# A graph layer with 12522 gathers of 128 rows: six stretches of them are cut to 112, 96, 64, 105, 98 and 80 rows

## The chip, the core and the metric

The kernel runs on one core of one Trainium2 chip. The time is the device time of that core in microseconds; the kernel before takes 17915.2 us (median of 2 runs, 17912.69 and 17917.71). Its profiled execution took 18022.0 us.

The engines are named as the profile names them: PE is TensorE (its weight loads are PEld), DVE is VectorE, ACT is ScalarE, POOL is GpSimd, and SP is SyncE, which here only issues transfers. A `q` behind a name is the queue in which an engine issues transfers.

## The reference

A graph of 50000 nodes has 1650000 edges, sorted by their destination; one edge of each node is a loop to itself. A node carries 160 numbers (64 scalars and 32 vectors of 3), an edge carries 4 (`sh`). For each edge the row of its source node is combined with the edge's four numbers and five small weight matrices, the results are summed over the edges of each destination, and the sum goes through two more matrices, a ReLU, a residual and a layer norm:

```python
ss, vv = (s[src], v[src])
e0 = sh[:, 0:1]
e1 = sh[:, 1:4]
dot = jnp.einsum('eui,ei->eu', vv, e1)
out0 = C0 * (ss * e0 @ W1 + dot * INV3 @ W2)
p3 = (ss @ W3)[:, :, None] * e1[:, None, :] * INV3
p4 = jnp.einsum('eui,uw->ewi', vv * e0[:, :, None], W4) * INV3
p5 = jnp.einsum('eui,uw->ewi', jnp.cross(vv, e1[:, None, :]), W5) * INV6
out1 = C1 * (p3 + p4 + p5)
m = jnp.concatenate([out0, out1.reshape(-1, 3 * MUL1)], axis=1)
m_agg = jax.ops.segment_sum(m, dst, num_segments=n)
...
return x + jax.nn.relu(h)          # h: m_agg through Ws and Wv
...
x = _layernorm(x + _L0_gnn_ref(...), axis=-1)
```

## The kernel before

Everything up to the ReLU is linear in the gathered rows, so the kernel first sums, for each node and each of the edge's four numbers, the number times the source's row (4 x 160 sums a node), and multiplies with one combined matrix `BWk` afterwards.

**Units, groups, pairs, chunks.** 128 edges are a unit. For each unit, POOL gathers the 128 source rows of 640 bytes from HBM into one slice of the tile `xg` (line 398), one index in each partition. Six units (`G`) are a group; the destinations of a group lie within 32 consecutive nodes (`W`), since the edges are sorted. Two groups are a pair: 12 gathers, one `xg` tile, one `ps` tile. There are four `xg` tiles (pool `rows`), so the first gather of a pair waits until PE has read the pair four before. Twenty groups (`SG`) are a chunk, 120 gathers: for a chunk the sources, destinations and numbers of its edges are loaded (`load`), transposed so that the edges of a unit lie across the partitions (`place`), and the destinations are taken relative to the first node of their group (`rel`). `place` also keeps the least and the largest `rel` of each chunk in `extremes`, for a check at the end that all lay within the 32 nodes.

**A pair.** VectorE compares `rel` with 0 to 31 (`hot`, line 419) and multiplies with the edge's four numbers (`ha`, line 422): a matrix of 128 edges by 4 x 32. PE multiplies it with the gathered rows (line 447) and adds up six units in `ps`; the trace counts two matmul passes for each unit. VectorE turns `ps` in blocks of 32 (line 462) and adds it to the sums of the current segment of nodes, `ring`, at a column that depends on the data (line 471). When the last group that can touch a block of 128 nodes is done, five matmuls with `BWk` (line 776) and the norm finish it.

**Loops.** From the 101st group on (`NH` = 100) the edges are not read from the inputs but from a table `edges` that the kernel writes ahead of use, without the loops: `pack` takes rows of 1185 edges, 128 rows at a time (11 packs), moves the loops out with predicated copies on VectorE, and stores what is left. The loops' share is added node by node (`ask_own`, `set_own`). `reach` says how far in the table a chunk reads.

**What sets the order.** The engines' programs are written out in order (`manual_schedule`): the loop over the pairs issues the 12 gathers of a pair, then its matmuls, and between these, after each, a share of the other work (blocks, the next chunk, packs). A chunk's loads are issued three pairs ahead of the chunk that stands before it (`LEAD`). `near` estimates the destination of a group's first edge from its place in the list; from it follow the segments, the windows and the pairs after which each block can be finished.

Before, a group's first edge is simply `g * G * P`, 768 edges a group. The lines of the loads in the six stretches, of the gathers and of the matmuls are these:

Of the kernel before, what the change touches and what calls it, by code (L numbers as in the profile page):

```python
# [44 lines left out]
ALU = mybir.AluOpType  # L45
AX = mybir.AxisListType
# [4 lines left out]
P = 128  # L51
MUL0, MUL1 = 64, 32
D = MUL0 + 3 * MUL1
NK = 4
# [9 lines left out]
W = 32  # L64
# [4 lines left out]
SG = 20  # L69
# [10 lines left out]
ASK, OWN, QS, RUN = 8, 16, 8, 2  # L80
LEAD = 3

def plan(n_nodes, n_edges):

    nblk = 125
    assert n_nodes % nblk == 0
    assert W == FB
    nb = n_nodes // nblk
    again = 9

    per_unit = P * n_nodes / n_edges
# [10 lines left out]
    assert eh + (rows - 1) * row - n_nodes + eh * n_nodes / n_edges - far >= ngroups * group * P  # L102
    units = P * math.ceil(max(math.ceil(n_edges / P) + again - 1, math.ceil((eh + rows * row + 1) / P)) / P)
    return nblk, nb, again, group, units, ngroups, row, head, rows, far


@with_exitstack
def tile_gnn_resnorm(ctx: ExitStack, tc: tile.TileContext, x, src, dst, attr, W1, W2, W3, W4, W5, Ws, Wv, out, n_edges):
    nc = tc.nc
    N = x.shape[0]  # L110
    NBLK, NB, GA, G, NU, NG, L, NH, NR, FAR = plan(N, n_edges)
    EH = NH * G * P
    degree = n_edges / N

# [98 lines left out]
    cuts = sorted({0, NH, NG} | {round(i * NG / 10 / SG) * SG for i in range(10)})  # L213
# [5 lines left out]
    NSC = math.ceil(NG / SG)  # L219
    part_of = [next(i for i, (g0, g1) in enumerate(parts) if g0 <= s * SG < g1) for s in range(NSC)]  # L220
    off_of = [offs[i] for i in part_of]
    low = [max(math.floor(near(g)) - off_of[g // SG] - 1, 0) for g in range(NG)]
# [9 lines left out]
    with tc.tile_pool(name="once", bufs=1) as once, tc.tile_pool(name="raw", bufs=2) as rawp, \  # L232
# [20 lines left out]
        dq = nc.sync  # L253
# [3 lines left out]
        def load(s):  # L257

            g0 = s * SG
            ng = min(NG, g0 + SG) - g0  # L260
            u0, f0 = (g0 * G, g0) if s + 1 < NSC else ((g0 + ng) * G - P, g0 + ng - W)
            at = (g0 * G - u0, g0 - f0, ng)

            def fetch(to, what, c):

                rows = what.rearrange("(u i q) -> i u q", u=P // RUN, i=NK)
                dq.dma_start(to.rearrange("p (b r) q -> p b (r q)", r=RUN), rows)

            def fetch_first(to, what, c):

                firsts = what.rearrange("(g q) -> g q", g=W)[:, 0:1]
                with nc.allow_non_contiguous_dma(reason="one number of each group"):
                    dq.dma_start(to, firsts.unsqueeze(0).to_broadcast([NK, W, 1]))

            if g0 >= NH:
                C = 2 + NK
                if s * SG > NH:
                    f0 = g0 + ng - W
                    at = (at[0], g0 - f0, ng)
                p0, q0 = u0 * P - EH, f0 * G * P - EH  # L280
                r6 = rawp.tile([P, NK * W * C], F32, name="r6").rearrange("p (b e c) -> p b e c", b=NK, c=C)
                fd = rawp.tile([P, 1], F32, name="fd")
                fetch_first(fd, edges[0, q0 * C + 1:(q0 + W * G * P) * C + 1], C)
                fetch(r6.rearrange("p b e c -> p b (e c)"), edges[0, p0 * C:(p0 + P * P) * C], C)
# [61 lines left out]
        def place(cast_):  # L346
# [28 lines left out]
            if s:  # L375
# [15 lines left out]
        def gather(s, placed, u, n):  # L391
# [4 lines left out]
            begun_tiles[0] += 1  # L396
            for j in range(n):
                part = nc.gpsimd.indirect_dma_start(  # L398
                    out=xg[:, j, :], out_offset=None, in_=x,
                    in_offset=bass.IndirectOffsetOnAxis(ap=placed[0][:, u + j:u + j + 1], axis=0))  # L400
# [5 lines left out]
                rows.append((xg[:, j, :], filled[t][j], 16 * gathers[t][j], key))  # L406
            return rows

        idle, sent = [], []
# [32 lines left out]
        def group_sums(p, rows, ha):  # L442
# [1 line left out]
            ps = psA.tile([P, PG, D], F32, name="ps")  # L444
            fresh("ps")
            for j, (xr, sem, count, key) in enumerate(rows):
                mm = nc.tensor.matmul(ps[:, j // G, :], ha[:, j].rearrange("p k w -> p (k w)"), xr,  # L447
                                      start=j % G == 0, stop=j % G == G - 1)
                mm.wait_op(sem, count, "sem-ge")
                tc.declare_no_dep(mm.ins, group=key, reason="its own semaphore is waited for")  # L450
# [23 lines left out]
        C = 2 + NK  # L474
# [442 lines left out]

        def reach(s):

            end = min(NG, (s + 1) * SG) * G * P  # L920
            if s * SG < NH:
                return 0
            if s + 1 < NSC:
                end = max(end, (s * SG * G + P) * P)
            if s * SG == NH:
                end = max(end, (s * SG + W) * G * P)
            return end - EH

        packs, due = [], []
# [235 lines left out]
```

## Time and profile before

| | |
|---|---|
| time | 17915.2 us (median of 2 runs) |
| profiled execution | 18022.0 us, span 18020.3 us |
| POOL busy | 11866.1 us, 66% of the span |
| VectorE busy | 7478.3 us, 41% |
| PE busy, weight loads busy | 6860.2 us (38%), 6095.4 us (34%) |
| mean granted TensorE clock | 0.627 |
| gathers | 12522, mean 947 ns |
| transfer engines, the gathers' queue | 1026.60 MB, 23.5% of 16 engines' span |
| groups, pairs, chunks | 2087, 1044, 105 |

A group's row in the profile gives line, engine, operation and tiles (written <- read), the count, then busy time, the mean of one in ns, and the idle time of the engine just before these instructions with what ended most of it. "issue" means that the engine waited for nothing that the profile shows; "remote" that it was released by something that the profile does not show. A row of waits gives the total in us, how often, and the longest. A row of a timeline gives start and duration in us, and in square brackets the idle time before.

### The profile page before, as it was taken

The page shows a single profiled execution, that of the slowest core. Times are in us where ns is not written, and L with a number is a line of the kernel's source. Part 1 is how long each engine was busy: PE and PEld are TensorE (multiplying, and loading weights), DVE is VectorE, ACT ScalarE, POOL GpSimd, SP SyncE. Part 2 cuts the span into 40 slices and gives each one's busy share as a digit, 9 for nine tenths or more (in the row PEclk, how much of TensorE's full clock was granted, in tenths as well). Part 3 has the DMA queues.
Part 4 walks back from the last instruction along what each step waited for, and adds up shares of the span by engine and source line. Part 5 has one row for each costly group of instructions (what it writes and reads, how often), then busy time and mean ns, then how long its engine had stood idle before and what let it go on. Part 6 is the DMA issues. An engine that isn't in the chain of part 4 may idle for free. (4 is left out here: it accounts for less than half of the span.)

```text
span 18020.3 us, 93561 instructions
## 1 busy us (share of the span) xinstructions
PE 6860.2 (38%) x28971; PEld 6095.4 (34%) x28972; DVE 7478.3 (41%) x12038; ACT 171.6 (1%) x273; POOL 11866.1 (66%) x12535
## 2 busy tenths in 40 slices
PE   3333334333333333333333333333333333333433
PEld 2233333333333333333333333333333333333333
DVE  7344245334524442453344345434433452444232
ACT  0000000000000000000000000000000000000000
POOL 6566666666666666666666666666666666666666
PEclk6666666666666666666666666666666666666666
DMA  2222322322332233223223322332232233222222
GB/s 72 79 71 78 79 68 73 83 76 70 77 81 70 71 80 77 70 73 85 73 70 78 80 70 72 82 77 69 72 85 74 69 76 78 72 70 71 75 72 61
DMA packets 740962, 1341.57 MB, mean 74 GB/s; under 512 B 243310, under 2 KB 522674, under 8 KB 725894
## 3 DMA queue, kind: packets, MB, share of 16 engines
q0 software_dynamic: 601056, 1026.60, 23.5%
q1 hardware_dynamic: 138138, 308.06, 5.6%
q8 instruction: 231, 3.78, 0.1%
q14 instruction: 273, 2.24, 0.0%
q10 hardware_dynamic: 1264, 0.88, 0.0%
HBM read 1263.28 MB, written 71.42 MB: 74 GB/s over the span
## 5 line engine op out<-in xcount | busy, mean ns | idle before, releaser
L398 POOL DMA_INDIRECT xg<-in_x,si x12522 | 11862.6, 947 | 6108.8 <-issue 3663.5
L447 PE MATMUL ps<-xg,ha 128*128 128x160 f32 x25044 | 6282.8, 397 | 9643.7 <-issue 5600.4
L447 PEld LDWEIGHTS ps<-xg,ha 128*128 128x128 f32 x25044 | 5409.4, 267 | 10356.9 <-issue 10352.3
L462 DVE STREAM_TRANSPOSE sums<-ps 128x320 f32<-128x320 f32 x1044 | 527.0, 505 | 6249.8 <-remote 4712.4
L422 DVE TENSOR_TENSOR ha<-hot,pk 128x1536 f32<-128x1536 f32 x1044 | 1830.4, 1753 | 52.1 <-remote 11.0
L776 PE MATMUL phb<-BWk,ring 128*128 128x160 f32 (+1 forms) x3910 | 1176.4, 381 | 1441.0 <-issue 858.6
L184 DVE SCALAR_TENSOR_TENSOR y<-phb,xt 128x320 f32<-128x320 f32 x196 | 95.9, 489 | 3623.2 <-PE ps L447 2504.7
L776 PEld LDWEIGHTS phb<-BWk,ring 128*128 128x128 f32 (+1 forms) x3910 | 894.1, 258 | 1489.1 <-issue 886.9
L471 DVE TENSOR_TENSOR ring<-ring,sums 128x160 f32 x2087 | 684.5, 328 | 253.1 <-issue 158.6
L419 DVE TENSOR_TENSOR hot<-bank,rel 128x384 f32<-128x384 f32 x1044 | 570.6, 547 | 67.4 <-DMA xt<-in_x 67.3
L632 DVE COPY_PREDICATED prow<-marks,prow 128x2370 f32<-128x2370 int32 (+5 forms) x198 | 550.3, 2780 | 1.1
L766 DVE STREAM_TRANSPOSE ring<-xr 128x1280 f32<-128x1280 f32 x188 | 437.2, 2326 | 0.1
L632 DVE COPY_PREDICATED pra<-marks,pra 128x1580 f32<-128x1580 int32 (+5 forms) x198 | 378.8, 1913 | 0.0
L763 DVE TENSOR_TENSOR xr<-xr,bank 128x1280 f32<-128x1280 f32 x188 | 276.5, 1471 | 4.6 <-DVE bank L756 1.4
L194 ACT ACTIVATE rstd<-mv,eps_t 128x2 f32<-128x2 f32 x196 | 58.0, 296 | 16997.5 <-DVE mv L189 12612.7
L468 DVE TENSOR_TENSOR ring<-ring 128x196 f32<-128x196 f32 (+20 forms) x485 | 149.4, 374 | 1.8
L200 DVE TENSOR_SCALAR o<-y,mv,rstd 128x160 f32<-128x160 f32 x391 | 130.2, 374 | 10.9 <-remote 1.6
L629 DVE COPY_PREDICATED_SCALAR hit<-marks,none 128x395 int32 (+5 forms) x198 | 130.1, 657 | 10.9 <-DVE pri L627 3.2
L716 DVE MEMSET ring<- 128x1280 f32 (+1 forms) x98 | 119.3, 1218 | 23.1 <-issue 21.0
L188 DVE BATCH_NORM_STATS2 st<-y 128x6 f32<-128x160 f32 x391 | 121.7, 311 | 6.7
L630 DVE COPY_PREDICATED hit<-marks,pri 128x395 int32<-128x395 int32 (+5 forms) x198 | 118.5, 598 | 10.4 <-issue 2.2
L627 DVE TENSOR_TENSOR pri<-hit,marks 128x395 int32<-128x395 int32 (+11 forms) x198 | 113.5, 573 | 14.8 <-issue 3.2
(346 smaller groups left out, 1752.7 us busy)
## 6 DMA issues: line engine op xcount, KB each, us to landing
xg<-in_x,si POOLq DMA_INDIRECT x12522
xr<-in_x SPq DMA_DIRECT2D x93, 1280.0 KB
r<-edges SPq DMA_DIRECT2D x100, 384.0 KB
edges<-prow SPq DMA_DIRECT2D x1330, 27.8 KB
xt<-in_x SPq DMA_DIRECT2D x195, 160.0 KB
out<-o SPq DMA_DIRECT2D x195, 160.0 KB
pra<-in_attr SPq DMA_DIRECT2D x10, 2370.0 KB
selves<-mine SPq DMA_DIRECT2D x1328, 0.8 KB
```

The source lines that it names most:

```text
L200: nc.vector.tensor_scalar(o[:n, i], y[:n, i], mv[:n, i, 0:1], rstd[:n, i:i + 1], op0=ALU.subtract, op1=ALU.mult)
L398: part = nc.gpsimd.indirect_dma_start(out=xg[:, j, :], out_offset=None, in_=x, in_offset=bass.IndirectOffsetOnAxis(ap=placed[0][:, u + j:u ...
L419: idle[:] = [nc.vector.tensor_tensor(hot[:, :n], slotsP[:, 0:W].unsqueeze(1).to_broadcast([P, n, W]), rel[:, u:u + n].unsqueeze(2).to_broa ...
L422: nc.vector.tensor_tensor(ha[:, :n], hot[:, :n].unsqueeze(2).to_broadcast([P, n, NK, W]), pk[:, :, u:u + n].rearrange("p k u -> p u k").un ...
L447: mm = nc.tensor.matmul(ps[:, j // G, :], ha[:, j].rearrange("p k w -> p (k w)"), xr, start=j % G == 0, stop=j % G == G - 1)
L462: nc.vector.transpose(at[:, :ng], ps[:, :ng].rearrange("p g (b f) -> p g b f", f=FB))
L468: nc.vector.tensor_tensor(ring[k][:, b, :past], ring[k][:, b, :past], ring[k - 1][:, b, S:S + past], op=ALU.add)
L471: nc.vector.tensor_tensor(here, here, at[:, i], op=ALU.add)
L632: nc.vector.copy_predicated(what[:n, a:e], mi[:, r].unsqueeze(2).to_broadcast([n, e - a, what.shape[2]]), what[:n, a + d:e + d])
L763: nc.vector.tensor_tensor(xr[:, r], xr[:, r], sumP[:, r].unsqueeze(2).to_broadcast([P, r.stop - q, D]), op=ALU.mult)
L766: nc.vector.transpose(here[:, r], xr[:, r].rearrange("p q (b f) -> p q b f", f=FB))
L776: wrote("misc", nc.tensor.matmul(ph[:nb], ring[k][:, i, cols], BWk[:, i, :], start=i == 0, stop=i == ND - 1))
```

## The change

Of the chunks 8 to 14, 18 to 24, 28 to 34, 38 to 44, 48 to 54 and 58 to 64, a gather takes 112, 96, 64, 105, 98 and 80 edges in place of 128, on the first so many partitions; all other chunks keep 128. A group there has six times so many edges. The edges that these groups no longer take go to later groups: there are now 2320 groups, 1160 pairs, 116 chunks and 13920 gathers. `starts` holds each group's first edge. A short chunk's edges are loaded in two transfers: one for the full blocks of 32 edges in a unit, one for the rest (with edges behind the unit's end, which no one reads). The matmuls take the same first partitions; the one-hots and their products are still made for all 128.

```diff
+SIZES = (112, 96, 64, 105, 98, 80)
+
+
+def size_of(s):
+    i, j = divmod(s - 8, 10)
+    return SIZES[i] if 0 <= i < len(SIZES) and j < 7 else P
...
-    ngroups = math.ceil((n_edges - n_nodes + eh * n_nodes / n_edges + far) / (group * P))
...
+    starts = [0]
+    while starts[-1] < n_edges - n_nodes + eh * n_nodes / n_edges + far:
+        g = len(starts) - 1
+        starts.append(starts[-1] + group * (P if g < head else size_of(g // SG)))
...
     def near(g):
-        p = g * G * P
+        p = starts[g]
...
+        nc.vector.memset(extremes, 0.0)
...
             def fetch(to, what, c):
 
+                if size[s] < P:
+                    m = size[s] // W
+                    for i, what_ in ((slice(0, m), what[0:P * size[s] * c]), (slice(m, NK), what[m * W * c:])):
+                        by_unit = what_.rearrange("(u q) -> u q", u=P)[:, 0:(i.stop - i.start) * W * c]
+                        dq.dma_start(to[i.start * W:i.stop * W], by_unit.rearrange("u (i q) -> i u q", q=W * c))
+                    return
...
-            nc.vector.tensor_reduce(extremes[:, 0, s:s + 1], rel[:, :n], axis=AX.X, op=ALU.min)
-            begun.append(nc.vector.tensor_reduce(extremes[:, 1, s:s + 1], rel[:, :n], axis=AX.X, op=ALU.max))
+            nc.vector.tensor_reduce(extremes[:size[s], 0, s:s + 1], rel[:size[s], :n], axis=AX.X, op=ALU.min)
+            begun.append(nc.vector.tensor_reduce(extremes[:size[s], 1, s:s + 1], rel[:size[s], :n], axis=AX.X, op=ALU.max))
...
                 part = nc.gpsimd.indirect_dma_start(
-                    out=xg[:, j, :], out_offset=None, in_=x,
-                    in_offset=bass.IndirectOffsetOnAxis(ap=placed[0][:, u + j:u + j + 1], axis=0))
+                    out=xg[:size[s], j, :], out_offset=None, in_=x,
+                    in_offset=bass.IndirectOffsetOnAxis(ap=placed[0][:size[s], u + j:u + j + 1], axis=0))
...
-                mm = nc.tensor.matmul(ps[:, j // G, :], ha[:, j].rearrange("p k w -> p (k w)"), xr,
+                mm = nc.tensor.matmul(ps[:, j // G, :], ha[:xr.shape[0], j].rearrange("p k w -> p (k w)"), xr,
```

What this does to the order shows on POOL first. Before, its program is these rows from the end of the start-up on, nearly all in one run of gathers (`128x160` is partitions by numbers, `x` how many stand in a row):

```order
L803 IOTA quarter 128x4
L999 IOTA place 128x1185
L398 DMA xg<-in_x,si 128x160 x49
L505 IOTA at 1x1408
L398 DMA xg<-in_x,si 128x160 x12473
```

Now, from the same place up to the end of the third short stretch (line 398 has become 420):

```order
L825 IOTA quarter 128x4
L1021 IOTA place 128x1185
L420 DMA xg<-in_x,si 128x160 x49
L527 IOTA at 1x1408
L420 DMA xg<-in_x,si 128x160 x911
L420 DMA xg<-in_x,si 112x160 x840
L420 DMA xg<-in_x,si 128x160 x360
L420 DMA xg<-in_x,si 96x160 x840
L420 DMA xg<-in_x,si 128x160 x360
L420 DMA xg<-in_x,si 64x160 x840
```

Each short stretch is 840 gathers, with 360 full ones up to the next; the other three follow in the same way, and 6120 full ones stand at the end.

SP is the other engine whose program changes its form. At the load of chunk 8, the first short one, it had before (`fd` holds the destinations of the groups' first edges, `r` the chunk's edges, `xt` the node rows of two blocks, `sa` and `xr` what the loops need):

```order
L875 DMA out<-o 128x320
L273 DMA fd<-edges 128x1x1
L267 DMA r_4696<-edges 128x2x384
L709 DMA xt<-in_x 128x320
L746 DMA sa<-selves 128x1x64
L746 DMA xr<-in_x 128x1x2560
```

and now:

```order
L897 DMA out<-o 128x320
L295 DMA fd<-edges 128x1x1
L286 DMA r_4683<-edges 96x4x192
L286 DMA r_4683<-edges 32x4x192
L731 DMA xt<-in_x 128x320
L768 DMA sa<-selves 128x1x64
L768 DMA xr<-in_x 128x1x2560
```

The one transfer of the edges has become two, in runs of 192 numbers in place of 384, and what follows it stands one transfer later.

More of the change, by code (lines that the diff above doesn't have):

```diff
@@ L100, in plan @@
     rows = math.ceil((n_edges - eh) / row) + 2
-    ngroups = math.ceil((n_edges - n_nodes + eh * n_nodes / n_edges + far) / (group * P))
-    assert eh + (rows - 1) * row - n_nodes + eh * n_nodes / n_edges - far >= ngroups * group * P
+    starts = [0]
+    while starts[-1] < n_edges - n_nodes + eh * n_nodes / n_edges + far:
+        g = len(starts) - 1
+        starts.append(starts[-1] + group * (P if g < head else size_of(g // SG)))
+    assert size_of((len(starts) - 2) // SG) == P and len(starts) - 1 > head + SG
+    assert eh + (rows - 1) * row - n_nodes + eh * n_nodes / n_edges - far >= starts[-1]
     units = P * math.ceil(max(math.ceil(n_edges / P) + again - 1, math.ceil((eh + rows * row + 1) / P)) / P)
-    return nblk, nb, again, group, units, ngroups, row, head, rows, far
+    return nblk, nb, again, group, units, starts, row, head, rows, far
 @with_exitstack
@@ L110, in tile_gnn_resnorm @@
     N = x.shape[0]
-    NBLK, NB, GA, G, NU, NG, L, NH, NR, FAR = plan(N, n_edges)
+    NBLK, NB, GA, G, NU, starts, L, NH, NR, FAR = plan(N, n_edges)
+    NG = len(starts) - 1
     EH = NH * G * P
@@ L212, in tile_gnn_resnorm @@
     S = SB * P
-    cuts = sorted({0, NH, NG} | {round(i * NG / 10 / SG) * SG for i in range(10)})
+    cuts = sorted({0, NH, NG} | {round(i * NG / 10 / SG) * SG for i in range(10)}
+                  | {g for g in range(NH, NG, SG) if size_of(g // SG) != size_of(g // SG - 1)})
     parts = list(zip(cuts, cuts[1:]))
@@ L219, in tile_gnn_resnorm @@
     NSC = math.ceil(NG / SG)
+    size = [P if s * SG < NH else size_of(s) for s in range(NSC)]
     part_of = [next(i for i, (g0, g1) in enumerate(parts) if g0 <= s * SG < g1) for s in range(NSC)]
@@ L279, in load @@
                     at = (at[0], g0 - f0, ng)
-                p0, q0 = u0 * P - EH, f0 * G * P - EH
+                p0, q0 = (starts[g0] - EH + (u - g0 * G) * size[s] for u in (u0, f0 * G))
                 r6 = rawp.tile([P, NK * W * C], F32, name="r6").rearrange("p (b e c) -> p b e c", b=NK, c=C)
                 fd = rawp.tile([P, 1], F32, name="fd")
-                fetch_first(fd, edges[0, q0 * C + 1:(q0 + W * G * P) * C + 1], C)
-                fetch(r6.rearrange("p b e c -> p b (e c)"), edges[0, p0 * C:(p0 + P * P) * C], C)
+                fetch_first(fd, edges[0, q0 * C + 1:(q0 + W * G * size[s]) * C + 1], C)
+                fetch(r6.rearrange("p b e c -> p b (e c)"), edges[0, p0 * C:(p0 + P * size[s] + size[s] % P // W * W) * C], C)
                 return s, at, None, None, fd, r6[:, :, :, 0:2].rearrange("p b e c -> p c b e"), r6[:, :, :, 2:]
@@ L405, in gather @@
                 tc.add_to_no_dep_group(key, part.ins)
-                rows.append((xg[:, j, :], filled[t][j], 16 * gathers[t][j], key))
+                rows.append((xg[:size[s], j, :], filled[t][j], 16 * gathers[t][j], key))
             return rows
@@ L918, in reach @@
         def reach(s):
-            end = min(NG, (s + 1) * SG) * G * P
+            end = starts[min(NG, (s + 1) * SG)]
             if s * SG < NH:
@@ L923, in reach @@
             if s + 1 < NSC:
-                end = max(end, (s * SG * G + P) * P)
+                end = max(end, starts[s * SG] + P * size[s] + size[s] % P // W * W)
             if s * SG == NH:
-                end = max(end, (s * SG + W) * G * P)
+                end = max(end, starts[s * SG] + W * G * size[s])
             return end - EH
```

## The prediction

> **What bounds the kernel now.** I read the page first (busy shares, groups by line), then the waits of POOL, then its timeline, to see what one gather costs, and last the table by stretch, to see whether that price holds everywhere.
>
> ```profile
> span 18020.3 us, 93561 instructions
> PE 6860.2 (38%) x28971; PEld 6095.4 (34%) x28972; DVE 7478.3 (41%) x12038; ACT 171.6 (1%) x273; POOL 11866.1 (66%) x12535
> L398 POOL DMA_INDIRECT xg<-in_x,si x12522 | 11862.6, 947 | 6108.8 <-issue 3663.5
> L447 PE MATMUL ps<-xg,ha 128*128 128x160 f32 x25044 | 6282.8, 397 | 9643.7 <-issue 5600.4
> ```
>
> POOL is the busiest engine, and all that it does is 12522 gathers. Their busy time and the idle time before them make 11862.6 + 6108.8 = 17971.4 us, the whole span but 49. So the span is a chain of gathers, and the question is what one costs. The waits of POOL divide the idle part:
>
> ```profile
> POOL xg L398 <- issue: 3663.5, 12020, 1.7
> POOL xg L398 <- PE ps L447: 1220.3, 220, 33.2
> POOL xg L398 <- remote: 1201.7, 275, 6.9
> ```
>
> The first row is a gap that stands before nearly every gather, 3663.5 / 12020 = 0.305 us, with nothing waited for. The other two are waits for a free row buffer: 495 of them, 2422.0 us together, about 4.9 us each. Per gather that is 0.947 us of work, 3663.5 / 12522 = 0.293 of gap and 2422.0 / 12522 = 0.193 of waiting, in all 1.433 us. The timeline of POOL and PE shows both kinds:
>
> ```profile
> 9008.31 0.43 PE L447 MATMUL ps<-xg,ha 128*128 128x160 f32 x1 [2.37 <-issue]
> 9008.74 0.95 POOL L398 DMA_INDIRECT xg<-in_x,si  x1 [0.30 <-issue]
> 9009.99 0.95 POOL L398 DMA_INDIRECT xg<-in_x,si  x1 [0.30 <-issue]
> ...
> 9011.11 0.42 PE L447 MATMUL ps<-xg,ha 128*128 128x160 f32 x1 [2.38 <-issue]
> 9011.24 0.95 POOL L398 DMA_INDIRECT xg<-in_x,si  x1 [0.30 <-issue]
> 9012.49 0.95 POOL L398 DMA_INDIRECT xg<-in_x,si  x1 [0.30 <-issue]
> ...
> 9013.91 0.42 PE L447 MATMUL ps<-xg,ha 128*128 128x160 f32 x1 [2.38 <-issue]
> ...
> 9017.42 4.86 PE L447 MATMUL ps<-xg,ha 128*128 128x160 f32 x12 [0.98 <-issue]
> ...
> 9020.04 0.94 POOL L398 DMA_INDIRECT xg<-in_x,si  x1 [6.60 <-PE ps L447]
> ```
>
> POOL issues a gather each 1.25 us. PE meanwhile does a matmul pass only each 2.80 us, waiting for nothing that the trace shows; it falls behind, POOL runs out of buffers at 9013.4 and stands 6.60 us, and while POOL stands PE goes at 4.86 / 12 = 0.41 us a pass. What slows PE while gathers run the trace does not say. What can be read is how evenly it costs: the table by stretch (per engine busy and count; POOL is the fifth pair).
>
> ```profile
> 3000.00:6000.00 3000.00, 1138.59 (x4836) 1014.85 (x4836) 1224.21 (x1978) 29.62 (x45) 1983.90 (x2097) 0.63 0.29 75
> 9000.00:12000.00 3000.00, 1150.68 (x4838) 1015.14 (x4837) 1242.69 (x1971) 19.67 (x39) 1986.85 (x2097) 0.63 0.30 76
> 12000.00:15000.00 3000.00, 1167.63 (x4858) 1036.83 (x4859) 1291.57 (x2054) 29.64 (x45) 1982.49 (x2096) 0.63 0.29 74
> ```
>
> 2097, 2097 and 2096 gathers in 3000 us, 1.431 us each, though VectorE had 1224 us of work in the first stretch and 1292 in the last. The waits behave like a price per gather, not like the price of some other job that meets it now and then.
>
> **The change part by part.**
>
> *More gathers.* Six stretches of seven chunks of 120 gathers, 840 gathers each, 5040 in all, take 112, 96, 64, 105, 98 and 80 rows. They lack 16 + 32 + 64 + 23 + 30 + 48 = 213 rows a gather against 128, so 840 x 213 = 178920 edges need room elsewhere, 178920 / 128 = 1398 gathers. The new program indeed has 13920 where the old one has 12522, and 2320 groups where it had 2087; the rows gathered are 1602840 against 1602816, the same. At 1.433 us each, 1398 gathers are **+2003 us**, if a short gather costs what a full one does.
>
> *Does it?* The durations of all gathers (min/median/max in ns):
>
> ```profile
> L398 POOL DMA_INDIRECT xg<-in_x,si x12522: 940/946/2256, 5.5 to 17987.7; - x199
> ```
>
> All of these have 128 rows; no other size is in the trace. The bounds are therefore wide. From above: the 0.946 us is a fixed price and a short gather saves nothing. From below: it is all paid by the row, and a gather of 64 takes 0.473 us; then the missing rows save 1398 x 0.947 = 1324 us, and the sum is +679. The 0.293 us gap stands before the work and I take it as fixed. I take the upper end, since the nearest row, that of the gathers themselves, is flat over different indices, different load beside it and the whole span, which is how a price looks that hangs on the instruction. This is my weakest step, and both ends stay in the range.
>
> [...]
>
> *The waits in the six stretches.* 5040 x 0.193 = 973 us of them would lie there. Bounds: all of it stays (or grows, if PE falls further behind), or all of it goes because whatever slows PE hangs on the rows or bytes moved. The stretch table shows one price per gather; I take that it stays.
>
> *More pairs, chunks and matmuls on the other engines.* 233 more groups are 116 more pairs. For each pair VectorE builds one-hots and turns sums:
>
> ```profile
> L462 DVE STREAM_TRANSPOSE sums<-ps 128x320 f32<-128x320 f32 x1044 | 527.0, 505 | 6249.8 <-remote 4712.4
> L422 DVE TENSOR_TENSOR ha<-hot,pk 128x1536 f32<-128x1536 f32 x1044 | 1830.4, 1753 | 52.1 <-remote 11.0
> L471 DVE TENSOR_TENSOR ring<-ring,sums 128x160 f32 x2087 | 684.5, 328 | 253.1 <-issue 158.6
> L419 DVE TENSOR_TENSOR hot<-bank,rel 128x384 f32<-128x384 f32 x1044 | 570.6, 547 | 67.4 <-DMA xt<-in_x 67.3
> ```
>
> 0.505 + 1.753 + 2 x 0.328 + 0.547 = 3.46 us a pair, 116 x 3.46 = 401 us in all, on an engine that is busy 41% of the span: each pair gives it 17.2 us (12 gathers), and POOL's own issue covers 15 of these. I cost it at nothing; uncovered it would be +401. If a gather of 64 fell to half, a pair would take 12 x (0.473 + 0.293) = 9.2 us, still above VectorE's 3.46, but below PE's 24 passes at 0.397 = 9.5: there PE would begin to count. The 2796 more matmul passes (2 x 1398) lie in the same place, beside POOL, and their delay is what the 0.193 us already holds.
>
> *Loads.* A chunk of the six stretches fetches its edges in two transfers of half the run length instead of one, and there are 11 more chunks. The transfers that concern this (count and KB each; packets, MB and share of the 16 transfer engines):
>
> ```profile
> r<-edges SPq DMA_DIRECT2D x100, 384.0 KB
> q1 hardware_dynamic: 138138, 308.06, 5.6%
> q0 software_dynamic: 601056, 1026.60, 23.5%
> ```
>
> One of them in the timeline of SP's queue, with the transfer behind it:
>
> ```profile
> 8960.63 0.55 SPq L267 DMA_DIRECT2D r<-edges  x1
> 8961.22 0.51 SPq L709 DMA_DIRECT2D xt<-in_x  x1
> ```
>
> The second transfer holds SP for another half microsecond, 42 times; behind it in SP's queue stand the node rows and the selves of later blocks. The chunk's first reader comes four pairs (4 x 17.2 = 69 us) after the issue, and the queue holds the transfer engines 5.6% of the time, so I take nothing; uncovered it would be 42 x 0.55 = 23 us. The memset of the extremes runs once, and the reductions over fewer partitions are as many as before. No wait is added.
>
> *Sum.* +2003 us against the profiled execution's own 18022.0 us. The runs' median is 17915.2, 0.9941 of that, so the change is +1991 there: 17915 + 1991 = 19906, which I round to **19900 us**, 11% slower.
>
> **The rivals.**
>
> A is the forecast: every gather costs 1.433 us whatever its rows. 0.55.
>
> B, the short gathers free PE: POOL's work stays at 0.947, but with fewer rows moved PE is not slowed and the waits vanish in the six stretches. For it: PE runs fast exactly when POOL stands (the timeline above). Against: it also runs fast in other pairs while gathers go on, and nothing shows that rows matter. 2003 - 973 = 1030, times 0.9941 is +1024: 18940. 0.15.
>
> C, POOL pays by the row, in part or in whole, and the waits stay or partly go: from 0.3 of the full saving (-397, about 19510) to the whole of it (+679, 18590). For it: 128 rows are 128 addresses that something has to compute. Against: the flat row. If the price went in steps by the rows that each of the 16 transfer engines gets, 8 for 128 rows, 7 for 112, 105 and 98, 6, 5 and 4 for 96, 80 and 64, the saving would be 840 x 0.947 x (3 + 2 + 3 + 4) / 8 = 1193 us in place of 1324, 18720. 0.18. [...]
>
> D, the sizes that are no multiple of 16 are dearer: a remainder handled by another path, priced by the nearest row at one more gap of 0.305 us for 1680 gathers, +512 on top: 20415. Nothing in the profile speaks for or against. 0.07.
>
> E, the other side: rows set the pace. What holds the chain at 1.43 us is then not the instruction but moving 128 rows of 640 bytes and all that hangs on it: work, gap and wait all shrink with the rows. The rows in all are unchanged (1602840), so the time is too: 17915. It decides if a gather of 64 comes every 0.72 us. For it: the evenness of the stretch table fits it as well. Against: the transfer queue of the gathers holds the engines only 23.5% of the span, and 0.30 us of gap before every gather would have to shrink with the rows of the one behind it. 0.05.
>
> **How the numbers follow.** 0.55 + 0.15 + 0.18 + 0.07 + 0.05 = 1. The likeliest case gives 19900. The range runs from 18900, just below B, to 20250, 350 above the forecast, for waits that grow and half of D. Outside lie E (0.05), the lower half of C (0.09) and half of D (0.03): 0.17. A change of 2% is 358 us, and that is about what a measurement of this kernel can tell from no change. Slower by more needs only that a short gather does not cost in proportion: A, B, C and D, less 0.01, so 0.94. Within 2%: E, less a part, 0.04. Faster by over 2%: work in proportion and no waits at all (2003 - 1324 - 973 = -294) would still be -1.6%; it needs the gap to shrink besides, 0.02.
>
> **What would show it.** In the new trace the six runs of 840 short gathers can be found by their place in the order (from gather 960, 2160, 3360, 4560, 5760 and 6960 on). There the duration of a gather decides A against C: 946 ns in all six, or shorter with the rows. The step from 112 to 105 and 98 decides C's two forms and D. The gathers per 3000 us decide B: 2097 as before, or 3000 / 1.25 = 2400. The prediction is wrong if the mean of a gather in the stretch of 64 is well below 0.9 us, or if the waits of POOL there drop below half of 0.193 us a gather.

## The result and the profile after

The changed kernel takes **19889.9 us** (median of 2 runs, 19887.08 and 19892.69) against 17915.2: a ratio of 1.110, 95% interval 1.106 to 1.115. The forecast was 19900, within 18900 to 20250. The profiled execution took 19887.08 us.

Lines move by 22: the gather now stands in line 420, the matmul in 469, `ha` in 444, the turn of the sums in 484. The page first (span, POOL's and PE's groups: count, busy, mean ns, idle time ahead of them), then the waits of POOL (us in total, times, longest):

```profile
span 19885.3 us, 101789 instructions
...
L420 POOL DMA_INDIRECT xg<-in_x,si x13920 | 13116.3, 942 | 6714.5 <-issue 4086.6
L469 PE MATMUL ps<-xg,ha 128*128 128x160 f32 (+6 forms) x27840 | 7205.4, 406 | 10498.6 <-issue 6318.8
```

```profile
POOL xg L420 <- issue: 4086.6, 13378, 4.3
POOL xg L420 <- PE ps L469: 1444.8, 263, 28.7
POOL xg L420 <- remote: 1172.1, 272, 7.9
```

13116.3 + 6714.5 = 19830.8, again the whole span but 55 us. Per gather that is 0.942 of work, 4086.6 / 13920 = 0.294 of gap and 2616.9 / 13920 = 0.188 of waiting, in all 1.424 us, where it was 0.947, 0.293 and 0.193. The number of gathers went up by 1398, and the price of one hardly moved.

How the price is made up did move. The durations of the gathers in the six stretches of 112, 96, 64, 105, 98 and 80 rows, and in the rest of full ones behind them (min/median/max in ns, first and last start):

```profile
L420 POOL DMA_INDIRECT xg<-in_x,si x840: 920/927/1103, 1424.8 to 2612.1; - x168
...
L420 POOL DMA_INDIRECT xg<-in_x,si x840: 907/913/1287, 3126.8 to 4319.8; - x168
...
L420 POOL DMA_INDIRECT xg<-in_x,si x840: 895/902/1101, 4832.6 to 6019.9; - x168
...
L420 POOL DMA_INDIRECT xg<-in_x,si x840: 942/959/1120, 6541.6 to 7726.5; - x168
...
L420 POOL DMA_INDIRECT xg<-in_x,si x840: 942/959/1194, 8243.8 to 9434.5; - x168
...
L420 POOL DMA_INDIRECT xg<-in_x,si x840: 893/900/1156, 9951.3 to 11137.6; - x168
...
L420 POOL DMA_INDIRECT xg<-in_x,si x6120: 942/949/1911, 11146.1 to 19845.1; - x198
```

And the same stretches in the table by stretch, for the gathers alone (length of the stretch, POOL busy and count, granted clock, share of the transfer engines, GB/s):

```profile
1424.80:2613.00 1188.20, 780.98 (x840) 0.61 0.27 69
3126.80:4320.70 1193.90, 768.82 (x840) 0.60 0.25 60
4832.60:6020.80 1188.20, 759.75 (x840) 0.50 0.18 43
6541.60:7727.40 1185.80, 802.75 (x840) 0.61 0.24 59
8243.80:9435.50 1191.70, 803.13 (x840) 0.59 0.23 56
9951.30:11138.50 1187.20, 758.43 (x840) 0.53 0.21 50
11146.00:19846.00 8700.00, 5814.67 (x6120) 0.62 0.29 74
```

Divide each row by its count. Work is 0.930, 0.915, 0.904, 0.956, 0.956, 0.903 and 0.950 us. The pace, length by count, is 1.415, 1.421, 1.415, 1.412, 1.419, 1.413 and 1.422 us. The gather of 64 rows needs 0.051 us less of POOL than that of 105, and yet the two come at a pace that differs by 0.003 us. That is no difference: seven pieces of 1200 us among the full gathers at the end hold 840 to 848 of them, a pace of 1.415 to 1.429 us. The waits of POOL (us, times) in the stretch of 64 rows, and below them in that of 105:

```profile
  remote: 96.9, 21
  PE ps L469: 80.3, 16
```

```profile
  PE ps L469: 76.7, 14
  remote: 62.9, 13
```

They are 177.2 and 139.6 us: 37.6 us more of waiting where there are 43.0 us less of work. So POOL does not set the pace here: something else hands out about 1.42 us a gather, 17.0 us a pair, and POOL's waits fill what its work leaves.

### The profile page after: what moved, and what is told of

The parts are those of the page before. It is cut to its first block, busy times and chain, and to the rows that moved or that the text cites. A ratio compares the mean times of both kernels' runs of the same rounds, so it can differ in the third digit from the quotient of the medians.

```text
span 19885.3 us, 101789 instructions
## 1 busy us (share of the span) xinstructions
PE 7800.6 (39%) x31767; PEld 6883.4 (35%) x31768; DVE 7899.5 (40%) x12773; ACT 171.3 (1%) x273; POOL 13119.8 (66%) x13933
## 5 line engine op out<-in xcount | busy, mean ns | idle before, releaser
L420 POOL DMA_INDIRECT xg<-in_x,si x13920 | 13116.3, 942 | 6714.5 <-issue 4086.6
L469 PE MATMUL ps<-xg,ha 128*128 128x160 f32 (+6 forms) x27840 | 7205.4, 406 | 10498.6 <-issue 6318.8
L469 PEld LDWEIGHTS ps<-xg,ha 128*128 128x128 f32 (+6 forms) x27840 | 6196.7, 274 | 11345.3 <-issue 11341.6
L484 DVE STREAM_TRANSPOSE sums<-ps 128x320 f32<-128x320 f32 x1160 | 586.6, 506 | 7645.5 <-remote 5216.4
L444 DVE TENSOR_TENSOR ha<-hot,pk 128x1536 f32<-128x1536 f32 x1160 | 2034.6, 1754 | 48.9 <-remote 5.5
L493 DVE TENSOR_TENSOR ring<-ring,sums 128x160 f32 x2320 | 760.0, 328 | 306.1 <-issue 196.2
L441 DVE TENSOR_TENSOR hot<-bank,rel 128x384 f32<-128x384 f32 x1160 | 633.5, 546 | 64.3 <-DMA xt<-in_x 63.0
L490 DVE TENSOR_TENSOR ring<-ring 128x216 f32<-128x216 f32 (+35 forms) x485 | 148.6, 373 | 2.4 <-issue 1.0
L738 DVE MEMSET ring<- 128x1270 f32 (+1 forms) x98 | 118.5, 1210 | 22.9 <-issue 21.5
L395 DVE STREAM_TRANSPOSE pk<-r 128x512 f32<-128x512 f32 x116 | 121.4, 1046 | 2.6 <-DMA r<-in_attr 2.6
```

The lines of the kernel that those rows point to most:

```text
L420: part = nc.gpsimd.indirect_dma_start(out=xg[:size[s], j, :], out_offset=None, in_=x, in_offset=bass.IndirectOffsetOnAxis(ap=placed[0][:si ...
L441: idle[:] = [nc.vector.tensor_tensor(hot[:, :n], slotsP[:, 0:W].unsqueeze(1).to_broadcast([P, n, W]), rel[:, u:u + n].unsqueeze(2).to_broa ...
L444: nc.vector.tensor_tensor(ha[:, :n], hot[:, :n].unsqueeze(2).to_broadcast([P, n, NK, W]), pk[:, :, u:u + n].rearrange("p k u -> p u k").un ...
L469: mm = nc.tensor.matmul(ps[:, j // G, :], ha[:xr.shape[0], j].rearrange("p k w -> p (k w)"), xr, start=j % G == 0, stop=j % G == G - 1)
L484: nc.vector.transpose(at[:, :ng], ps[:, :ng].rearrange("p g (b f) -> p g b f", f=FB))
L490: nc.vector.tensor_tensor(ring[k][:, b, :past], ring[k][:, b, :past], ring[k - 1][:, b, S:S + past], op=ALU.add)
```

## The experiments

Two theories stood against each other after this. **P**, the prediction's form: work, gap and waiting are three prices that add up. **S**: a steady pace of about 17 us a pair is set elsewhere, and the waits are what is left over. The runs fell on several chips, and the kernel before took quite different times on them, which turned out to be part of the answer:

| runs | kernel before on that chip |
|---|---|
| the prediction's | 17915.2 us |
| e1 to e4 | 18007.5 us |
| e5 to e8 | 15755.3 us |
| e9, e10 | 15716.0 us |
| e11 | 15752.5 us |
| e12 | 17923.3 us |

All ratios below are to the kernel before on the same chip.

**e1: more work on POOL.** One memset ahead of each pair's gathers:

```diff
+            nc.gpsimd.memset(idle_work, 0.0)       # 128 x 640
             rows = gather(s, placed[s], (g - s * SG) * G, ng * G)
```

> The kernel before with one more instruction on POOL ahead of each pair's 12 gathers: it fills 128 x 640 numbers that nobody reads, an estimated 1 to 1.5 us a pair by the gap of 0.305 us and a microsecond of work. Theory 1 (the pace of 1.42 us a gather is set at PE, and POOL's waits are only what is left of it): POOL's waits shrink by what is added and the time stays within 1% (17900 to 18100). Theory 2 (the chain of the prediction: work, gap and wait add up on POOL): 1044 pairs x 1 to 1.5 us are added, 18950 to 19500, and the waits stay at 0.19 us a gather.

Measured: 18612.2 us, ratio 1.034 (1.032 to 1.035). It does not test what it was meant to. POOL's instructions are not part of the hand-written order, and the memsets were put far ahead of the pairs that they were written for:

```profile
L970 POOL MEMSET idle_work<- x1044: 622/632/732, 1.7 to 1322.6; 128x640 f32 x174
```

All 1044 ran within the first 1322.6 us. There they cost about their own time (1044 x 0.633 = 661, measured +605); in the rest of the run nothing had changed. The 456 gathers that stand among these memsets waited for buffers for 17.0 us, 0.04 us each in place of 0.19, and the run is up by 574 to 638 us (95% interval), a little less than the memsets took; that speaks for S, but only as far as so few waits can. Beyond this the run leaves the price of one memset and the lesson to look where an added instruction lands.

**e2: half the matmul passes.** `ha` in bf16, and the rows read as the upper halves of their numbers, so that each product is taken with rounded numbers and PE needs one pass a unit, not two (12522 passes in the profile, 25044 before):

```diff
-            ha = op.tile([P, PG * G, NK, W], F32, name="ha")
+            ha = op.tile([P, PG * G, NK, W], BF16, name="ha")
...
-                mm = nc.tensor.matmul(ps[...], ha[...], xr, ...)
+                mm = nc.tensor.matmul(ps[...], ha[...], xr.bitcast(BF16).rearrange("p (f h) -> p f h", h=2)[:, :, 1], ...)
```

> The kernel before with the gathers' matmuls in bfloat16: the one-hot products are written as bfloat16 and PE reads the upper half of each gathered number, so that a unit takes one weight load and one pass in place of two (the numbers are thereby rounded). Theory 1: PE no longer sets the pace, the waits of POOL go, a gather comes each 1.25 us, 15700 to 16000. Theory 2: POOL's work and gap stay, and its waits have no cause in the number of passes: 17500 to 17950. VectorE writes half the bytes of the products, which neither theory counts.

**e3: shorter passes.** Five of the six matmuls of a group take 32 of the 160 columns; the sums of the other columns leave out those units:

```diff
+                cols = slice(0, W if j % G else D)
-                mm = nc.tensor.matmul(ps[:, j // G, :], ha[...], xr,
+                mm = nc.tensor.matmul(ps[:, j // G, cols], ha[...], xr[:, cols],
```

> The kernel before with as many matmuls as before, but five of the six of each group over 32 of the 160 numbers (the rest of the sums is left out). If theory 1 holds and it is the time of PE's work that counts, the time falls as with one pass, to 15700 to 16300; if it is the number of PE's instructions, it stays near 17900. Theory 2: 17900.

**e4: a fifth row buffer.**

```diff
-... tc.tile_pool(name="rows", bufs=4) as rowp
+... tc.tile_pool(name="rows", bufs=5) as rowp
-            t = begun_tiles[0] % 4
+            t = begun_tiles[0] % 5
```

with five sets of semaphores, and the pool `ahead` cut from 3 to 2 buffers for the room.

> The kernel before with five row buffers in place of four (and two in place of three buffers for the node rows, to make room). If PE falls behind only now and then and is fast enough on the whole, 15 us more of slack swallow most waits of 5 us: 16000 to 17000. If PE's side is a steady limit of 17.1 us a pair (theory 1 in its strict form), one more buffer is filled once and nothing is won: within 1% of 17915. Theory 2 says the same as the strict form if the waits are a price of each gather.

Measured, on one chip: e2 17858.5 us, ratio 0.992 (0.990 to 0.994); e3 18007.6, 1.000 (0.999 to 1.001); e4 18017.0, 1.001 (1.000 to 1.002). PE's group in e2 and the waits of POOL in e2 and e4:

```profile
L447 PE MATMUL ps<-xg,ha 128*128 128x160 bf16 x12522 | 2272.9, 318 | 12879.3 <-DVE ha L422 6022.9
```

```profile
POOL xg L398 <- remote: 1615.7, 296, 10.2
POOL xg L398 <- PE ps L447: 502.4, 90, 47.3
```

```profile
POOL xg L398 <- PE ps L447: 1203.8, 216, 33.9
POOL xg L398 <- remote: 1187.5, 287, 6.9
```

PE's matmuls fell from 6282.8 to 2272.9 us, and POOL still waits for 2118 us in place of 2422 (the first profile is the only one of the kernel before). A fifth buffer leaves 2391, the shorter passes 2426. So the waits are neither PE's throughput nor a lack of buffers.

**e5 and e6: work on POOL, held in its place.** POOL joins the hand-written order, and two or six memsets stand ahead of each pair:

```diff
-        ...manual_schedule(engines={ET.SP, ET.PE, ET.DVE, ET.Activation})
+        ...manual_schedule(engines={ET.SP, ET.PE, ET.DVE, ET.Activation, ET.Pool})
...
+            for _ in range(2):                      # e6: range(6)
+                nc.gpsimd.memset(idle_work, 0.0)    # 128 x 640
             rows = gather(s, placed[s], (g - s * SG) * G, ng * G)
```

> Two memsets of 128 x 640 on GpSimd ahead of the twelve gathers of each pair, now held in that place; a memset of this size took 0.633 us in the run before, so about 1.27 us a pair, 1320 us in all. The waits of POOL in the kernel before are 2422 / 1044 = 2.32 us a pair, more than that. If a steady pace of about 17.1 us a pair is set elsewhere and POOL's waits only fill what its own work leaves (theory S), the time stays (ratio 0.995 to 1.01) and the waits fall from 0.193 to about 0.09 us a gather. If work, gap and waits are three prices that add up, as the prediction had it (theory P), it is about 1320 us more: ratio 1.07.

> Six such memsets a pair, about 3.80 us, more than the 2.32 us of waits. Theory S: the waits go to nearly nothing and the rest shows, (3.80 - 2.32) x 1044 = 1545 us more, ratio about 1.086. Theory P: 3.80 x 1044 = 3970 us more, ratio about 1.22.

**e7: `ha` two pairs ahead.** A fourth `ha` buffer, and the one-hots of pair p + 2 in place of p + 1:

```diff
-                if j == 3 and p + 1 < len(pairs):
-                    s1, g1, ng1 = pairs[p + 1]
-                    has[p + 1] = spread(...)
+                if j == 3 and p + 2 < len(pairs):
+                    s1, g1, ng1 = pairs[p + 2]
+                    has[p + 2] = spread(...)
```

> The one-hots and ha of a pair are built two pairs ahead in place of one (a fourth ha buffer), so that TensorE no longer waits for ha behind the sums of the pair before on VectorE. If the loop from TensorE's sums over VectorE's ha back to TensorE sets the 17.1 us a pair (theory L), hot and ha (0.547 + 1.753 us) leave a loop that spans two pairs: 1.15 us a pair less, about 1200 us, ratio 0.93. If the pace is set by something that does not run over VectorE, the ratio stays within 0.99 to 1.01.

Measured: e5 17000.3 us, ratio 1.079 (1.077 to 1.081); e6 19868.8, 1.261 (1.259 to 1.264); e7 15755.2, 1.000 (0.999 to 1.001). These three could not tell P from S, because the chip on which they ran has no waits to fill: the kernel before takes 15755.3 us there, 1.258 us a gather. The waits of POOL in e7, whose time is that of the kernel before, and below them those of PE in e7:

```profile
POOL xg L398 <- issue: 3595.8, 11792, 0.3
POOL xg L398 <- PE ps L447: 182.6, 599, 0.3
```

```profile
PE ps L447 <- DMA xg<-in_x,si: 5302.5, 9052, 8.3
```

No wait of POOL for PE is longer than the 0.3 us gap, and PE waits for the rows of the gather just issued. On the prediction's chip the waits of PE in the kernel before read otherwise:

```profile
PE ps L447 <- issue: 5600.4, 2943, 24.0
PE ps L447 <- DVE ha L422: 3280.4, 462, 61.0
```

There PE stands for up to 24.0 us at a time for nothing that the profile shows. But by the profile's times PE is no longer at work on the buffer that POOL waits for. These are, in the kernel before, the 24 passes of one pair, the turn of its sums on VectorE, and the gather that is the first to use the pair's buffer again:

```profile
9033.17 5.01 PE L447 MATMUL ps<-xg,ha 128*128 128x160 f32 x24 [4.93 <-issue]
9070.95 0.52 DVE L462 STREAM_TRANSPOSE sums<-ps 128x320 f32<-128x320 f32 x1 [26.35 <-PE ps L447]
9071.19 0.94 POOL L398 DMA_INDIRECT xg<-in_x,si  x1 [6.46 <-PE ps L447]
```

The last of the passes ends at 9038.18. VectorE is free from 9044.60 on, and it and POOL go on together, 32.8 us after the passes. (The passes, turns and gathers were paired by their order in the program; the name in square brackets is only that of the pass nearest in time.) Over the whole run 606 of the turns began more than 0.5 us after the end of the instruction that VectorE had begun before them, and half of these came 18.8 us or more after the pair's last pass. POOL stood for more than 0.5 us before 477 first gathers of a pair; half of these came 21.9 us or more after the last pass on their buffer. In the changed kernel VectorE's figure is 19.0 us (683 turns). On the chips without waits it is 0.04 us, in e7 (796 turns) and in e9 below (970). So with waits, what PE has done reaches the other engines late. Whether its passes end later than the profile has them (it models their ends), or the signal of their end comes late, these traces do not tell.

Where there are no waits, POOL's work adds up, as P has it: (17000.3 - 15755.3) / 1044 = 1.19 us a pair for two memsets of 0.641, and 3.94 for six:

```profile
L971 POOL MEMSET idle_work<- 128x640 f32 x2088 | 1337.7, 641 | 60.2
```

**e8: six other sizes.** The changed kernel with

```diff
-SIZES = (112, 96, 64, 105, 98, 80)
+SIZES = (127, 113, 120, 104, 88, 72)
```

> The changed kernel with 127, 113, 120, 104, 88 and 72 edges a gather in the six stretches: 840 x 144 / 128 = 945 more gathers than before, 13467. Theory S (a steady pace of 1.42 us a gather whatever the rows): 945 x 1.42 = 1340 us more than the kernel before, ratio about 1.075, each stretch at 1.41 to 1.43 us a gather, though POOL's work differs. [...]

Measured: 19617.3 us, ratio 1.245 (1.243 to 1.248), on the chip without waits. The table by stretch for the gathers (127, 113, 120, 104, 88, 72 rows, then full ones):

```profile
1216.60:3655.10 2438.50, 2137.05 (x840) 0.50 0.21 40
4106.60:6375.10 2268.50, 1980.62 (x840) 0.50 0.21 39
6826.80:7909.40 1082.60, 826.54 (x840) 0.56 0.31 80
8361.30:9444.30 1083.00, 826.91 (x840) 0.55 0.28 72
9896.50:10972.80 1076.30, 820.29 (x840) 0.51 0.25 63
11424.50:12471.90 1047.40, 791.23 (x840) 0.51 0.21 52
12471.90:19589.60 7117.70, 5388.90 (x5670) 0.58 0.33 84
```

Work is 2.544, 2.358, 0.984, 0.984, 0.977, 0.942 and 0.950 us: one row fewer than 128 costs 1.6 us a gather. The gathers' queue in the stretch of 127, and in the full ones at the end (packets, MB, share of 16 engines):

```profile
q0 software_dynamic: 268517, 74.68, 17.9%
```

```profile
q0 software_dynamic: 272096, 464.77, 26.8%
```

Per gather these are 320 packets and 88.9 KB for 127 rows, 48 packets and 82.0 KB for 128 (81.9 KB of rows). 127 rows are 81.3 KB; the 7.6 KB on top come to 1905 entries of 4 bytes, 15 x 127. The packets of the changed kernel's gathers above show what such entries stand for. A gather of 128 rows has 16 packets of 4480 bytes (7 rows) and 16 of 640, one of 112, 96, 80 or 64 rows has 16 of 4480, 3840, 3200 or 2560: 16 shares of 8, 7, 6, 5 and 4 rows. A gather of 105 rows has 15 packets of 4480 bytes and one of 28, one of 98 rows has 14 and two: 15 and 14 shares of 7 rows, and in place of the others what reads as 7 entries of 4 bytes. Every gather there has 16 more packets of 4 bytes. By this pattern 127 rows would be one share of 127 and 15 of as many entries without a row: 18 packets of 4480 bytes and one of 640, 270 of 28 bytes and 15 of 4, and the 16 more make the 320 packets, and 89.0 KB. The stretch of 113 fits one share too: between 4200 and 6300 us 223774 packets and 61.50 MB for 777 gathers are 288 packets and 79.2 KB each, as 113 rows and 15 x 113 entries would have. And inside the stretches of 120, 104 and 88 rows the queue's packets have a mean of 1602, 1391 and 1178 bytes, where 15, 13 and 11 shares of 8 rows with 1, 3 and 5 without would have 1602, 1390 and 1178. Whether each share is one transfer engine's, the traces do not tell. A gather of 127 rows came every 2438.50 / 840 = 2.90 us, and POOL's own 2.544 is nearly all of that.

Taken by rows per share, the sizes fall nearly into one line (64 rows, 4 a share, lie off it: they take 902 ns, where 80 rows, 5 a share, take 900). From 113 to 127, 14 more rows in the one share cost 0.186 us, 13 ns each; from 120 (15 shares of 8 rows, 0.984) to 127 it is 1.560 / 119, again 13 ns. From 64 (16 shares of 4 rows) to 128 (16 of 8) it is 949 - 902 = 47 ns in the stretches of the changed kernel above, 12 ns a row. And 112, 105 and 98 have shares of 7, but the two that have only 15 and 14 of these take 0.959 where 112 takes 0.927: 0.032 us where fewer than 16 shares hold rows, near the 0.027 to 0.034 by which 120, 104 and 88 (15, 13 and 11 shares of 8) stand above the full gather. The stretches of 127 and 113 take 2438.50 + 2268.50 = 4707 us where 1680 full gathers take 2109, two thirds of the 3862 us by which this kernel is slower.

**e9 and e10: the change again, and e5 again**, on another chip, which turned out to have no waits.

> The change itself again, beside the kernel before on the same chip. Where POOL waits for buffers as in the first profile (the kernel before near 18000 us): 1.42 us for each of 13920 gathers, ratio 1.110. Where it does not (the kernel before near 15755 us, 1.2555 us a gather): work and gap alone count. With 0.928, 0.915, 0.904, 0.956, 0.956 and 0.903 us for 112, 96, 64, 105, 98 and 80 rows as in the changed kernel's first profile, the six stretches have a mean of 0.927 us in place of 0.950, 5040 x 0.023 = 116 us less, and 1398 x 1.2555 = 1755 us more: +1640, ratio 1.104. If instead the short gathers save in proportion to their rows once no wait takes it back, 1755 - 1398 x 0.95 = 427 us more, ratio 1.027.

> The two memsets a pair again, beside the kernel before on the same chip. Where the kernel before waits some 2.3 us a pair: theory S (waits fill what POOL's own work leaves of a pace set elsewhere) ratio 0.995 to 1.01, theory P (prices that add up) 1.07. Where the kernel before has no waits, both give what the two memsets cost, ratio 1.079 as in the run before.

Measured: e9 17361.9 us, ratio 1.105 (1.102 to 1.108), the 1.104 that was worked out; e10 16962.3, 1.079 (1.076 to 1.082). The same stretches as above, now of e9:

```profile
1215.50:2249.70 1034.20, 778.00 (x841) 0.57 0.31 80
2700.70:3723.80 1023.10, 767.04 (x841) 0.54 0.29 71
4174.70:5188.80 1014.10, 758.03 (x840) 0.50 0.21 49
5640.10:6696.40 1056.30, 800.25 (x840) 0.55 0.27 66
7147.90:8204.20 1056.30, 800.32 (x840) 0.54 0.25 63
8655.20:9667.80 1012.60, 756.61 (x840) 0.52 0.24 57
9667.80:17333.50 7665.70, 5801.22 (x6120) 0.58 0.33 84
```

The work is that of the other chip within 0.005 us (0.925, 0.912, 0.902, 0.953, 0.953, 0.901, 0.948). But the pace follows it here: 1.230, 1.217, 1.207, 1.258, 1.258, 1.205 and 1.253 us, in each row the work and 0.305. What a short gather saves, 0.046 us for 64 rows, is kept here; on the chip with waits it is handed back as waiting.

**e11: e5 a third time**, on one chip alone.

> The two memsets a pair once more, sought beside a kernel before that waits (near 18000 us). There theory S (the waits fill what POOL's own work leaves of a pace set elsewhere) gives ratio 0.995 to 1.01 with the waits at about 0.09 us a gather, theory P (prices that add up) 1.07 with the waits at 0.18 to 0.19. Beside a kernel before near 15720 to 15755 us it can tell nothing new: ratio 1.079.

Measured: 16997.6 us, ratio 1.079 (1.076 to 1.082), once more without waits.

**e12: e5 and e7 in one kernel**, with six smaller memsets (128 x 160) for the room; the edits are theirs. The kernel before takes 17923.3 us on this chip, so here there are waits.

> Both edits in one kernel: six memsets of 128 x 160 a pair on GpSimd (by the size of the 128 x 640 one, 0.633 us, and of a 128 x 128 one, 0.205 us, about 0.23 us each, 1.4 us a pair) and the one-hots and ha built two pairs ahead. Beside a kernel before that waits (near 18000 us): if the waits fill what POOL's own work leaves of a pace set elsewhere and not over VectorE (theory S), ratio 0.995 to 1.01, waits down to 0.08 us a gather; if the loop over VectorE sets that pace (theory L), it falls by 1.15 us a pair and POOL's own 16.4 us become the bound, ratio about 0.96; if the prices add up (theory P), 1.4 x 1044 = 1460 us more, ratio 1.08, waits unchanged. Beside a kernel before near 15720 to 15755 us there are no waits to fill: ratio 1.08 to 1.09, and nothing is told apart.

Measured: 17885.9 us, ratio 0.998 (0.997 to 0.999). The timeline of POOL where no wait falls, POOL's waits for a buffer, and PE's for `ha`:

```profile
9019.70 1.69 POOL L972 MEMSET idle_work<- 128x160 f32 x6
9021.54 0.95 POOL L398 DMA_INDIRECT xg<-in_x,si  x1 [0.16 <-issue]
```

```profile
POOL xg L398 <- remote: 342.4, 186, 3.3
POOL xg L398 <- PE ps L448: 206.6, 86, 22.7
```

```profile
PE ps L448 <- DVE ha L423: 19.6, 2, 18.8
```

From the end of one gather (9019.70, where the memsets begin) to the start of the next there are 1.84 us in place of 0.30: 1.54 us more a pair, 1608 us in all. The time did not rise; the waits are 549.0 us, where the kernel before had 2422.0 in the first profile. P alone wants 1608 us more, a ratio of 1.09, and P with the loop over VectorE loosened (theory L, 1.15 us less a pair) still +0.39 x 1044 = 407 us, 1.023. L alone wants 0.96. Of the three at these prices only S holds. The run makes both edits at once, though, and e7 by itself was never run where there are waits: that the early `ha` took away 1.79 us of waiting a pair (2422.0 less 549.0, over 1044), in place of the 1.15 estimated, while the memsets added theirs as P has it, is not excluded by this run. The six stretches of the changed kernel, in which `ha` comes as it did before, are the evidence for S that stands without it. The pace itself is not set by the `ha` of a pair standing behind the sums: PE's waits for `ha` fell from 3280.4 to 19.6 us, and a pair still takes 17885.9 / 1044 = 17.1 us, with POOL standing 0.53 us of it.

## Why the prediction was right

*The gathers.* 13920, 1398 more, as counted; and their price all but unchanged, 1.424 us against 1.433. This was the likeliest case and it decided the time.

*"A short gather saves nothing."* The upper end was taken, 0.946 us; the row is 0.900 to 0.959. The step held because only a small part is paid by the row: with 12 to 13 ns for each row of a share (under e8), the 8 of a full gather are about 0.1 us of 0.947. It did not hold to the letter: 64 rows save 5%, 105 and 98 cost 1% more. Rival C had the right shape, steps by the rows per share, and a ninth of its size; C assumed that all 0.947 went that way (18720). Rival D had the right sign, and a tenth of its size: 0.032 us where fewer than 16 shares hold rows, priced at 0.305. That 112, 105 and 98 would cost alike, with seven rows each in C's steps, is not so in the rows (927 against 959 ns): the seven rows a share are in the packets of all three (4480 bytes; 16, 15 and 14 a gather), but the 0.032 us come on top.

*"The waits stay at 0.193 us a gather."* They are 0.188 over the run. This is the step whose reason was wrong. The prediction took them as a price of their own, added to the work. They are the rest of a pace set outside POOL: in the changed kernel they are larger where the work is smaller, and in e12, which also has the early `ha`, they shrink by about what POOL is given to do. Nor, by the profile's times, is it PE falling behind that makes POOL wait: the 6.60 us of waiting that the prediction shows end at 9020.04, and the last pass on that buffer had ended at 9014.3 (its row of 9013.91). With work almost fixed both readings give the same sum, so for this term the right number was luck; a change that made gathers cheaper by less than the waits would, by these rows, have saved hardly anything on that chip, where the prediction's form would have credited it in full.

*B, that the waits vanish in the short stretches* (2400 gathers in 3000 us): they do not; 3000 / 1.415 = 2120 in the stretch of 64, though the transfers moved 43 GB/s there and 74 in the full stretch behind. *E, that rows set the pace*: that stretch would go at 0.72 us a gather; it goes at 1.415.

*Cover.* VectorE's 116 more pairs, the matmuls, the second transfer: in e9, where POOL does not wait at all, each stretch is POOL's work and gap to within 0.001 us a gather, so they cost nothing there. With waits they cannot be seen apart.

*The scaling to the median.* The sum in profiled time was 18022.0 + 2003 = 20025, and the profiled execution took 19887: 138 too many, since the price fell by 0.01 us on 13920 gathers. The 107 us by which the profiled execution of before stood above its median made up for most of that. That the forecast is off by only 10 us is thus partly luck; without it the error is some 0.7%.

## What to carry to other kernels

A wait that looks like a price per instruction may be the rest of somebody else's pace: before it goes into a sum, ask whether it gets smaller when the waiting engine is given more to do. The number of indirect gathers counts here, hardly their rows (0.904 us of POOL for 64 rows, 0.950 for 128), so make full ones; where they must be short, multiples of 16 rows were best among the sizes run (0.903 to 0.930 us for 64, 80, 96 and 112 rows, 0.942 to 0.984 for 72, 88, 98, 104, 105 and 120), and 113 and 127 by far the worst (2.358 and 2.544). The ratio of this change to the kernel before on the same chip carried over from chip to chip (1.110 and 1.105), the waits behind it did not.

## What was not expected of the hardware

The same program takes 15716 to 15755 us on three of the chips and 17915 to 18008 us in the other sets of runs, about 14% apart. In the profiles of the longer runs PE stands for nothing that the profile shows (5600.4 us before the matmuls in the first one, 0.8 in e7), and what it has done reaches VectorE and POOL some 20 us late (under e5 to e7), which is when POOL waits. The rows of the gathers are not late: the last packet of a gather ends 2.27 us after the gather starts in the first profile and 2.28 us in e7 (medians). What causes it stays open: it is not the passes (e2, 0.992), their length (e3), the buffers (e4), the rows or bytes of a gather (the six stretches), POOL's own work or the early `ha` (e12). Not tested is what all the runs with waits have alike: twelve gathers a pair, and some ten signals a pair from PE (10582 on the passes in the first profile, for 1044 pairs). Their traces also lack most records of the gathers' landings (36736 records of landings in the first profile, 215148 in e7), so part of what they call "issue" and "remote" may be waits whose end was not recorded.

A gather of 127 rows keeps POOL 2.54 us and one of 113 rows 2.36, where 128 rows take 0.95 and 120 rows 0.98 (e8).
